# Query projection by seven half-block products in a fused cross-attention and state-space kernel (f32, one core)

## The chip, the cores and the metric

The kernel runs on one core of a Trainium2 chip. The metric is the device time of one execution in microseconds (us); lower is better. The engines have their own instruction streams: PE (TensorE matmuls; PEld is its weight load), DVE (VectorE), ACT (ScalarE), POOL (GpSimd) and SP (SyncE, which issues most DMAs). PE writes into PSUM banks of 128 partitions by 512 f32; ACT and DVE read them from there.

## The reference

One layer over x (4096 queries of width 512) and a context (3202 rows of width 512), with 8 heads of width 64, in f32:

```python
x = _layernorm(builder_state, g1, beta1)
base_n = _layernorm(base_state, g1, beta1)
# _mha: q, k, v = heads(x, Wq, bq), heads(kv, Wk, bk), heads(kv, Wv, bv)
#       attn = softmax(q k^T / sqrt(HD)); out = (attn v) @ W_o.T + b_o
x = residual + _mha(x, base_n, W_qkv, b_qkv, W_o, b_o)
residual = x
xn = _layernorm(x, g2, beta2)
U = (xn @ W_in.T + b_in) @ Bmat
# step: s = silu(s @ A.T) + u_t, over the 4096 steps
x = residual + einsum('tbs,sh->bth', states, Cmat)
return x + (program_probs.mean(axis=1) @ W_prog.T + b_prog)
```

The change concerns `heads(x, Wq, bq)` alone: the 512 by 512 projection of the normalised queries.

## The kernel before

**Stages.** A lead (function `lead`, up to about 200 us of the span) normalises and turns the context, makes all keys and values and stores them in HBM (`kd`, `vd`), and makes the queries of the first block. Then comes the attention over 8 blocks of QB = 512 queries (Q = 0 to 7). Last, a scan over the states runs in chunks, overlapping the last block's end (`drain`).

**A block.** `units` lists (Q, hp, half): hp is one of 4 pairs of heads (128 features), half is 256 queries of the block. A unit has NDC = 13 steps of 256 keys (the last has 128). A step is a set of scores (`scores`, line 1069: 16 matmul instructions of 64 by 64 weights and 256 columns; the array runs four of them side by side), an exponential on ACT (`weights`, line 1146, out into a p tile), a running sum for the denominators on DVE (`add`, line 1154) and, LAG = 4 steps later, a set of value products (`product`, line 1203, into two po banks; the last step has eight instructions more, line 1191). p tiles are a ring of NP = 18; a tile is given back when both its add and its value products are done. At a unit's end DVE folds the sum (1161), ACT swaps halves (1173), DVE gathers (1178), PE sums over partitions (`sums`, pd, 1231), ACT copies the denominators (1270), DVE inverts them (1275), scales the output (1286) and checks the inverse's sum (1278); `output` (ACT, 1248) and `join` (DVE, 1252) take the values out of the po banks. Each pair of heads begins with a bound on its scores from a sample of keys: `sample` (1089), `maximum` (1103), `spread` (1111, PE), `base` (1124, 1125, DVE) and `extra` (ACT, 1131); `rest` (1140, DVE) adds the extra keys to the sum.

**The queries of the next block.** `queries` loads the next 512 rows of x while block Q runs, normalises them, turns them on DVE (`flip`) and by 16 small DMAs on SP (`move`) into the tile `xn` (128 partitions, 4 parts of the 512 features, 512 queries). Four pieces of `heads` then follow, one for a pair of heads: four matmuls of 128 by 128 weights and 512 columns (line 333; f32 takes two instructions each, so 8), then one ACT operation (line 342) that scales, adds the bias and writes a tile of 128 by 512 in the ring `qp` of six. The tile `xn` is free for the next block when all four are done.

**The rows of a block that is done.** `project` makes the output projection (`outs`, pa, line 1446), the residual, the second layer norm and the state inputs (`inputs`, pu, line 1503) of each half block.

**What sets the order.** Nothing is ordered by hand inside the attention. `Plan` holds pieces, each with an engine, an assumed cost, the pieces it comes after, a due time and the rings it takes from and gives back to. `Plan.order` runs a list schedule over assumed costs and emits the pieces in that order; each engine then executes its own instructions strictly in that order, waiting on semaphores. PE's pieces are of two kinds: `"quarters"` (64 by 64 tiles of the array) and whole-array ones. The planner charges ENTER and LEAVE for a change of kind, and holds a lone whole-array piece back by ALONE. `PORT` names DVE's pieces that it keeps off POOL's. Two PSUM banks (`ps_m`, `ps_n`; ring `m` of two) serve the heads, the samples, the denominators, pa and pu in turn.

**Seven products exist already** in the lead: `Seven` (line 500) makes groups of keys and values with them. The sums of weights are made on POOL (`weight_sums`, line 708), the differences of the context tile on DVE (line 735) in four `qp` tiles, the banks are read by ACT (513, 517) and DVE (523).

Of the kernel before, what the change touches and what calls it, by code (L numbers as in the profile page):

```python
# [20 lines left out]
P = 128  # L21
# [20 lines left out]
NP = 18  # L42
# [28 lines left out]
class Plan:  # L71
# [12 lines left out]
    PORT = ("add", "rest", "fold", "gather", "scale", "t", "tied", "wk", "wv", "wq", "rowv")  # L84
# [107 lines left out]
def xattn_ssm_kernel(  # L192
# [118 lines left out]
    qp = actx.enter_context(tc.tile_pool(name="qp", bufs=6))  # L311
# [17 lines left out]
    def heads(Q, hp, xn, home=None):  # L329

        pq = home() if home else m_tile([P, 512], f"pq_{Q}_{hp}")
        for i in range(NC):
            nc.tensor.matmul(  # L333
                pq,
                wq[:, i, hp * P : (hp + 1) * P],
                xn[:, i, :],
                start=(i == 0),
                stop=(i == NC - 1),
            )
        yield  # L340
        t = qp.tile([P, QB], F32, tag="q", name=f"q_{Q}_{hp}")
        nc.scalar.activation(  # L342
            t, pq, AF.Identity, bias=bias[:, hp : hp + 1], scale=HD**-0.5
        )
        qt[Q, hp] = t
# [128 lines left out]
    def quarters(w):  # L474

        lo, hi = slice(0, QU), slice(QU, H)
        return w[:, :2, lo], w[:, 2:, lo], w[:, :2, hi], w[:, 2:, hi]

    class Seven:
# [11 lines left out]
        def product(self, k):  # L491
            if k == "1":
                self.x = self.bank("x")
            elif k == "2":
                self.y = self.bank("y")
            to, left, right = self.y if k in "235" else self.x, self.left[k], self.right[k]
            for b in range(2):
                of = slice(b * P, (b + 1) * P)
                for i in range(2):
                    nc.tensor.matmul(  # L500
                        to[:, b, :],
                        left[:, i, of] if self.of_keys else right[:, i, of],
                        right[:, i, :] if self.of_keys else left[:, i, :],
                        start=(k in "125" and b == 0 and i == 0),
                        stop=(i == 1),
                        skip_group_check=True,
                    )
# [48 lines left out]
    def lead():  # L556
# [3 lines left out]
            dict(cx=6, xh=3, fs=3, t=2, v=2, k=2, m=2, ct=2, q=6, ks=3, vs=3, w=2),  # L560
# [135 lines left out]
        def weight_sums(name, w, tags, after, due):  # L696

            a11, a12, a21, a22 = quarters(w)
            left = dict(zip("124", (a11, a12, a22)))
# [10 lines left out]
            for i, (k, x, y, op) in enumerate((  # L710
                ("5", a21, a22, ALU.add), ("6", "5", a11, ALU.subtract),
                ("7", a11, a21, ALU.subtract), ("3", a12, "6", ALU.subtract),
            )):
                first = {"6": "5", "7": "6", "3": "7"}.get(k)
                add(("s", name, k), "POOL", 1300, partial(sum_, k, x, y, op),
                    after + ([("s", name, first)] if first else []), due + i * 1300)
            return left

        def group(g, lefts):
# [3 lines left out]
            right = {}  # L723
# [4 lines left out]
            def sum_(k):  # L728
# [3 lines left out]
                t = qp.tile([P, QB], F32, tag="q", name=f"t{k}_{g}").rearrange("p (c k) -> p c k", c=2)  # L732
# [4 lines left out]
            for i, k in enumerate("5674"):  # L737
                first = {"6": "5", "4": "6"}.get(k)
                add(("t", g, k), "DVE", 690, partial(sum_, k),
                    halves[0] + halves[1] + ([("t", g, first)] if first else []), d + 3000 + i, ["q"],  # L740
                    [ct] + ([("q", ("t", g, first))] if first else []))
# [7 lines left out]
            for at_, (a, k) in enumerate(  # L749
# [10 lines left out]
                gives = [ct] if k in "123" else [("q", ("t", g, k))]  # L760
# [213 lines left out]
        for hp in range(FIRST):  # L974
            v, d = {}, start_of(n_g) + 10000 + 3000 * hp

            def head(hp=hp, v=v):
# [6 lines left out]
                [("x.copy", t) for t in range(NT)] + ["wq", "wq.bias"], d, ["m", "q"])  # L984
# [72 lines left out]
    sp_ = lctx.enter_context(tc.tile_pool(name="sp_", bufs=NP))  # L1057

# [297 lines left out]
    def queries(plan, Q, d):  # L1356
# [42 lines left out]
        head_pieces(plan, Q, range(NC), w, copied, d, QSTEP // 2, [("xn", of_xn)])  # L1399
# [7 lines left out]
    def head_pieces(plan, Q, hps, xn, copied, d, apart, xn_, ring="m"):  # L1407
# [4 lines left out]
        for hp in hps:  # L1412
# [6 lines left out]
            plan.add(("heads", Q, hp), "PE", 3600, head, copied, d, [ring, "q"], xn_)  # L1419
# [165 lines left out]
    def open_scan():  # L1585

        t = qp.tile([P, QB], F32, tag="q", name="c2")
# [330 lines left out]
    def unit(plan, i):  # L1918
# [17 lines left out]
        q = [("q", Q, hp)] if Q or hp >= FIRST else []  # L1936
        first = i if half == 0 else index[Q, hp, 0]
        if half == 0:
            d = (max(s0 - REF, 0) if i else -40) * STEP
            plan.add(("sample", i), "PE", 440, partial(sample, w), q, d, ["m", "m"],  # L1940
                     [("q", ("heads", Q, hp))], "quarters")
# [8 lines left out]
        for c in range(NDC):  # L1950
# [5 lines left out]
                     [("q", ("heads", Q, hp))], "quarters")  # L1956
# [24 lines left out]
    def drain(plan):  # L1981
# [14 lines left out]
        plan.add("c2", "SP", 200, open_scan, [("heads", NQB - 1, NC - 1)], a0 - 6 * STEP, ["xn", "q"])  # L1996
# [10 lines left out]
        for j in range(L):  # L2007
            plan.add(("fetch", j), "SP", 100, partial(fetch, j),
                     ["fetch", ("product", n, j // 2)], d + (5 + j / 2) * STEP, ["p"])
# [210 lines left out]
    with tc.manual_schedule():  # L2220
# [4 lines left out]
                s=2, m=2, mt=1, o=1, p=NP, acc=3, extra=4, q=6, x=2, x1=1, xn2=1, fs=4,  # L2225
                xn=1, xh=2, max=2, rd=2, o_=12,
            ),
            dict(q=[("heads", 0, hp) for hp in range(FIRST)], xn=["first"]),
        )
        head_pieces(plan, 0, range(FIRST, NC), first_xn, [("spread", 0)], -40 * STEP, 0, [("xn", "first")], "o")  # L2230
# [102 lines left out]
```

## Time and profile before

| | us |
|---|---|
| median of 3 runs | 1921.74 (1921.47 to 1922.03) |
| the profiled execution, its own time | 1919.92 |
| its span in the profile | 1918.0 |
| query heads, line 333, PE busy | 110.5 (248 instructions) |
| query reads, line 342, ACT busy | 21.3 (31) |
| scores and values, lines 1069 and 1203, PE busy | 839.7 and 838.8 |
| output projection, line 1446, PE busy | 107.0 |

How to read it: a group's row gives the source line, engine, operation, out<-in by tile names, partitions x elements, the count, then busy time and mean ns of one, then the idle time of the engine just before these instructions and what ended most of it. Matmuls are pipelined, so the rows of a timeline overlap by the last one's tail; the distance between two starts is the price of one in a stream. In a timeline a row gives start, length, engine, line and how many instructions were merged. Some records of matmuls are missing (a few per cent).

### The profile page before, as it was taken

To read this page: it belongs to the slowest core of one execution; us is meant where nothing else is said; L and a number is where in the kernel's file an instruction comes from. 1 tells how busy PE (TensorE), PEld (TensorE's weight loads), DVE (VectorE), ACT (ScalarE), POOL (GpSimd) and SP (SyncE) were. 2 spreads that over 40 slices of the span, in tenths; PEclk is the share of its full clock that TensorE was granted. 3 is DMA by queue.
4 is the path that set the end of the run, shared out by engine and by line. 5 is a ranking of instruction groups with operands and counts; after the bars stand their busy time and mean duration, and the time that the engine had idled before them with its cause. 6 is when DMAs were issued, how large, how long until landed. Compare 5 with 4: busy or idle time off the path is not lost.

```text
span 1918.0 us, 67581 instructions
## 1 busy us (share of the span) xinstructions
PE 1903.8 (99%) x29296; PEld 1318.5 (69%) x29296; DVE 1502.4 (78%) x2035; ACT 1173.6 (61%) x1647; POOL 231.5 (12%) x378
## 2 busy tenths in 40 slices
PE   9999999999999999999999999999999999999997
PEld 5887688666667666666667666766666666766675
DVE  6642697888868887788778887888788886978877
ACT  3242676676656666656667665666666765766653
POOL 6120000001100120011000120012001110011105
PEclk9999999999999999999999999999999999999999
DMA  7554232232422343223323342224322341545577
GB/s 253 160 155 123 61 105 58 69 103 77 107 71 82 93 125 88 82 75 108 88 59 93 85 126 75 82 87 120 87 68 87 88 123 54 151 117 145 174 191 230
DMA packets 260761, 207.47 MB, mean 108 GB/s; under 512 B 94632, under 2 KB 233896, under 8 KB 260460
## 3 DMA queue, kind: packets, MB, share of 16 engines
q1 hardware_dynamic: 256440, 196.48, 36.1%
q10 hardware_dynamic: 4020, 6.62, 1.2%
q8 instruction: 232, 3.80, 0.8%
q14 instruction: 69, 0.57, 0.1%
HBM read 156.32 MB, written 29.88 MB: 97 GB/s over the span
## 4 chain that ended last, share of the span: by engine, by line


## 5 line engine op out<-in xcount | busy, mean ns | idle before, releaser
L1146 ACT ACTIVATE p<-s,shifts 128x1024 f32<-128x1024 f32 (+1 forms) x832 | 893.1, 1082 | 477.7 <-PE s L1069 462.4
L1154 DVE TENSOR_TENSOR acc<-p,acc 128x1024 f32<-128x1024 f32 (+1 forms) x704 | 828.3, 1177 | 136.9 <-ACT p L1146 101.8
L1069 PE MATMUL s<-q,k 64*64 64x256 f32 x12800 | 839.7, 377 | 0.2 <-ACT p L1146 0.2
L1203 PE MATMUL po<-p,v 64*64 64x256 f32 x12800 | 838.8, 377 | 0.0
L1069 PEld LDWEIGHTS s<-q,k 64*64 64x64 f32 x12800 | 500.4, 133 | 199.2 <-ACT p L1146 15.0
L1203 PEld LDWEIGHTS po<-p,v 64*64 64x64 f32 x12800 | 497.9, 133 | 184.3 <-issue 17.3
L1275 DVE RECIPROCAL rd<-rd 128x256 f32<-128x256 f32 (+1 forms) x64 | 110.1, 1722 | 70.6 <-ACT rd L1270 70.6
L1440 POOL TENSOR_TENSOR xr<-xr,rowb 128x512 f32<-128x512 f32 x30 | 40.7, 1365 | 996.9 <-DMA k<-kd 422.6
L333 PE MATMUL pq<-xn,wq 128*128 128x512 f32 x248 | 110.5, 598 | 0.0
L1446 PE MATMUL pa<-wo,o 128*128 128x512 f32 x240 | 107.0, 599 | 0.0
L1154 DVE TENSOR_TENSOR acc<-p,p 128x1024 f32<-128x1024 f32 x64 | 80.3, 1254 | 10.2 <-ACT p L1146 9.9
L333 PEld LDWEIGHTS pq<-xn,wq 128*128 128x128 f32 x248 | 45.8, 190 | 55.8 <-issue 55.8
L1446 PEld LDWEIGHTS pa<-wo,o 128*128 128x128 f32 x240 | 44.4, 190 | 56.0 <-issue 56.0
L342 ACT ACTIVATE q<-pq,bias 128x512 f32<-128x512 f32 x31 | 21.3, 687 | 84.3 <-PE pq L333 84.3
L1178 DVE TENSOR_TENSOR acc<-swap,acc 64x256 f32<-64x256 f32 x126 | 55.3, 439 | 8.9 <-ACT swap L1173 7.2
L1140 DVE TENSOR_TENSOR acc<-x,acc 2x256 f32<-2x256 f32 x128 | 53.1, 415 | 2.6
L1173 ACT COPY swap<-acc 64x256 f32<-64x256 f32 x126 | 50.8, 404 | 6.9 <-DVE acc L1161 3.2
L1463 POOL TENSOR_TENSOR xr<-x,modb 128x512 f32<-128x512 f32 x30 | 38.2, 1273 | 121.4 <-DVE x L1459 121.4
L1161 DVE TENSOR_TENSOR acc<-acc 128x512 f32<-128x512 f32 x63 | 44.2, 701 | 1.4
L1336 POOL TENSOR_SCALAR rstd_x<-mv_x 128x1 f32<-128x1 f32 x28 | 6.2, 220 | 319.1 <-DVE mv_x L1333 317.5
L523 DVE TENSOR_TENSOR ks<-pky,ks 128x512 f32<-128x512 f32 x15 | 10.4, 692 | 43.6 <-PE pky L500 28.7
L517 ACT ACTIVATE ks<-pkx,bias 128x256 f32<-128x256 f32 x40 | 16.8, 471 | 43.1 <-PE pkx L500 31.6
(260 smaller groups left out, 1405.8 us busy)
## 6 DMA issues: line engine op xcount, KB each, us to landing
k<-kd SPq DMA_DIRECT2D x432, 128.0 KB, 2.5
v<-vd SPq DMA_DIRECT2D x432, 128.0 KB, 2.2
xn<-x SPq DMA_DIRECT2D x448, 32.0 KB, 1.9
xr<-in_x_dram SPq DMA_DIRECT2D x30, 256.0 KB, 3.2
x1d<-xr SPq DMA_DIRECT2D x30, 256.0 KB, 2.3
x<-in_x_dram SPq DMA_DIRECT2D x28, 256.0 KB, 3.7
cx<-in_ctx_dram SPq DMA_DIRECT2D x25, 256.0 KB, 4.9
kd<-ks SPq DMA_DIRECT2D x20, 256.0 KB, 2.3
```

What stands on the lines that cost most here:

```text
L333: nc.tensor.matmul(pq, wq[:, i, hp * P : (hp + 1) * P], xn[:, i, :], start=(i == 0), stop=(i == NC - 1),)
L1069: nc.tensor.matmul(s[k0 : k0 + HD, a, b, :], kts[(*w["at"][:2], c)][r, b * CK + k0 : b * CK + k0 + HD], q[r], start=True, stop=True, skip_ ...
L1140: nc.vector.tensor_tensor(to[r], t[r], to[r], ALU.add)
L1146: nc.scalar.activation(t[:, :, :nb, :], w["ps"][c][:, :, :nb, :], AF.Exp, bias=w["shift"])
L1154: nc.vector.tensor_tensor(w["acc"][:, :, :nb, :], t[:, :, :nb, :], before[:, :, :nb, :], ALU.add)
L1161: nc.vector.tensor_tensor(acc[:, :, 0, :], acc[:, :, 0, :], acc[:, :, 1, :], ALU.add)
L1173: nc.scalar.copy(w["swap"][r], of[(1 - k) * HD : (2 - k) * HD])
L1178: nc.vector.tensor_tensor(of[r], w["swap"][r], of[r], ALU.add)
L1203: nc.tensor.matmul(w["po"][k][a * HD : (a + 1) * HD, :QU], vts[Q, hp, c][r, b, a * HD : (a + 1) * HD], t[r, a, b, :], start=(c == 0 and b ...
L1275: nc.vector.reciprocal(w["rd"][:, part], (w["pd"] if last else w["rd"])[:, part])
L1440: nc.gpsimd.tensor_tensor(v["x"], v["x"], rowb, ALU.add)
L1446: nc.tensor.matmul(v["pa"], o_t[Q, c, half][:, t * P : (t + 1) * P], wo[:, c, :], start=(c == 0), stop=(c == NC - 1),)
```

## The change

For blocks Q = 1 to 7, the four pieces of `heads` become seven products of half size, one level of Strassen's scheme in Winograd's form. With a = the query weights in quarters (a11, a12: first two pairs of heads, by halves of the features; a21, a22: last two pairs), and b = `xn` in quarters (b11, b21: first 256 queries, by halves of the features; b12, b22: last 256):

- sums of weights, once, on POOL: s5 = a21 + a22, s6 = s5 - a11, s7 = a11 - a21, s3 = a12 - s6
- differences per block, on DVE: t5 = b12 - b11, t6 = b22 - t5, t7 = b22 - b12, t4 = b21 - t6; t7 overwrites b12 and t4 overwrites b21 in `xn`
- products in the order 1, 2, 6, 5, 7, 3, 4, into two banks: x gathers a11 b11, then s6 t6, s7 t7, a22 t4; y takes a12 b21, is begun anew with s5 t5, then gathers s3 b22
- after each product the bank is read out, before the next may write it: x after 1, 6, 4 and y after 5 by ACT (two operations of 128 by 256, with scale and bias), y after 2 and 3 and x after 7 by DVE (one operation that scales and adds onto the query tile in SBUF)

A product is four matmuls (eight instructions) of 128 by 128 weights and 256 columns. The query tiles become tiles of two pairs of heads (128 by 2 by 512), in a ring of three; the lead's differences share them two by two. Three tiles `alt` hold the weight sums (two) and t5, t6 (one), and later serve as rows 0 to 2 of the last stage; for them the ring of p tiles goes from 18 to 15. The two banks of ring `m` are held from product 1 to the last reads.

In the built order of instructions, PE's stream in the lead and behind the last block's queries is the same as before. In blocks three to eight the three heads that stood right behind pu are gone from there; products 1, 2 and 6 come where the fourth head stood, behind score set 5 of unit (3,0), then one value set, then 5, 7, 3 and 4. In block two the three heads stood by themselves, between value and score sets of unit (2,1); its products stand where the others do. On DVE t5, t6 and t7 stand near score sets 2 and 3 of unit (2,1), t4 and the three reads among the adds of unit (3,0). The load of Cmat for the scan (`c2`) comes 17 rows later on SP.

```diff
-NP = 18
+NP = 15
+NA = 3
...
-    qp = actx.enter_context(tc.tile_pool(name="qp", bufs=6))
+    qp = actx.enter_context(tc.tile_pool(name="qp", bufs=3))
...
+    def pair_of(Q, hp):
+        t = qp.tile([P, 2, QB], F32, tag="q", name=f"q_{Q}_{hp}")
+        for k in range(2):
+            qt[Q, hp + k] = t[:, k]
+        return t
...
+    def seventh(to, still, moving, start):
+        for b in range(2):
+            for i in range(2):
+                nc.tensor.matmul(
+                    to[:, b, :],
+                    still[:, i, b * P : (b + 1) * P],
+                    moving[:, i, :],
+                    start=(start and b == 0 and i == 0),
+                    stop=(i == 1),
+                    skip_group_check=True,
+                )
+
+    def left_sums(w):
+        a11, a12, a21, a22 = quarters(w)
+        return (
+            ("5", a21, a22, ALU.add), ("6", "5", a11, ALU.subtract),
+            ("7", a11, a21, ALU.subtract), ("3", a12, "6", ALU.subtract),
+        ), dict(zip("124", (a11, a12, a22)))
...
-        head_pieces(plan, Q, range(NC), w, copied, d, QSTEP // 2, [("xn", of_xn)])
+        by_sevenths(plan, Q, w, copied, d, ("xn", of_xn))
+
+    lefts = {}
+
+    def query_weights(plan, after, d):
+        sums, left = left_sums(wq)
+        lefts["q"], tiles = left, {}
+        def sum_(k, x, y, op):
+            if k in "57":
+                tiles[k] = parts_of(alt_tile("57".index(k), f"sq{k}"))
+            left[k] = tiles["57"[k in "73"]][k in "63"]
+            x, y = (left[z] if isinstance(z, str) else z for z in (x, y))
+            nc.gpsimd.tensor_tensor(left[k], x, y, op)
...
+    CHAIN = "1265734"
+    READS = {
+        "1": ("11", "ACT"), "2": ("11", "DVE"), "6": ("12", "ACT"), "5": ("22", "ACT"),
+        "7": ("22", "DVE"), "3": ("12", "DVE"), "4": ("21", "ACT"),
+    }
+
+    def by_sevenths(plan, Q, w, copied, d, of_xn):
...
+        def sum_(k):
...
+            x, y = {"5": (b12, right["1"]), "6": (b22, right["5"]), "7": (b22, b12), "4": (b21, right["6"])}[k]
+            nc.vector.tensor_tensor(right[k], x, y, ALU.subtract)
...
+            seventh(v["y" if k in "235" else "x"], left[k], right[k], k in "125")
+
+        def read(k):
+            m, n = READS[k][0]
+            of, cs = v["y" if k in "235" else "x"], slice((int(n) - 1) * QU, int(n) * QU)
+            t = to[m][:, :, cs]
+            if READS[k][1] == "DVE":
+                nc.vector.scalar_tensor_tensor(t, of, HD**-0.5, t, ALU.mult, ALU.add)
+                return
+            for b in range(2):
+                hp = (int(m) - 1) * 2 + b
+                nc.scalar.activation(
+                    t[:, b], of[:, b], AF.Identity, bias=bias[:, hp : hp + 1], scale=HD**-0.5
+                )
...
+        before = {"6": "1", "5": "2", "7": "6", "3": "5", "4": "7"}
+        needs = {"1": copied + [("sq", "3")], "2": copied + [(*key, "1")], "3": copied}
+        for at, k in enumerate(CHAIN):
+            after = needs.get(k, [("tq", Q, k)]) + ([("sevenths.read", Q, before[k])] if k in before else [])
+            gives = [("tq", ("tq", Q, "5"))] if k in "56" else [of_xn]
+            plan.add((*key, k), "PE", 1740, partial(product_, k), after,
+                     d + at - (plan.ALONE if at > 1 else 0),
+                     {"1": ["m", "m", "q"], "5": ["q"]}.get(k, []), gives)
...
-            rows[j] = sp_.tile([P, 2, H], F32, tag="s", name=f"row_{j}")
+            rows[j] = alt_tile(j, name) if j < NA else sp_.tile([P, 2, H], F32, tag="s", name=name)
```

More of the change, by code (lines that the diff above doesn't have):

```diff
@@ L83 @@
     ENDS = 2 * NC * NQB - 2
-    PORT = ("add", "rest", "fold", "gather", "scale", "t", "tied", "wk", "wv", "wq", "rowv")
+    PORT = ("add", "rest", "fold", "gather", "scale", "t", "tq", "tied", "wk", "wv", "wq", "rowv")
     SHIFT = {
@@ L495, in product @@
                 self.y = self.bank("y")
[L496 to L507, printed above, removed]
+            to, sides = self.y if k in "235" else self.x, [self.left[k], self.right[k]]
+            seventh(to, *(sides if self.of_keys else sides[::-1]), k in "125")
         def keep(self, k, half):
@@ L696, in weight_sums @@
         def weight_sums(name, w, tags, after, due):
[L698 to L699 removed]
+            sums, left = left_sums(w)
             tiles = {}
```

102 lines of the change are left out of this document (75 added, 27 removed).

## The prediction

> **What bounds the kernel now.** I read the page first, then the stretches of one block, then the instructions of TensorE (PE) in order of time.
>
> ```profile
> span 1918.0 us, 67581 instructions
> PE 1903.8 (99%) x29296; PEld 1318.5 (69%) x29296; DVE 1502.4 (78%) x2035; ACT 1173.6 (61%) x1647; POOL 231.5 (12%) x378
> ...
> L1146 ACT ACTIVATE p<-s,shifts 128x1024 f32<-128x1024 f32 (+1 forms) x832 | 893.1, 1082 | 477.7 <-PE s L1069 462.4
> L1069 PE MATMUL s<-q,k 64*64 64x256 f32 x12800 | 839.7, 377 | 0.2 <-ACT p L1146 0.2
> ...
> L333 PE MATMUL pq<-xn,wq 128*128 128x512 f32 x248 | 110.5, 598 | 0.0
> ...
> L1463 POOL TENSOR_TENSOR xr<-x,modb 128x512 f32<-128x512 f32 x30 | 38.2, 1273 | 121.4 <-DVE x L1459 121.4
> ...
> L517 ACT ACTIVATE ks<-pkx,bias 128x256 f32<-128x256 f32 x40 | 16.8, 471 | 43.1 <-PE pkx L500 31.6
> ```
>
> PE is busy in 99% of the span. Its two largest users wait 0.2 us in all for others, whereas ScalarE's exponentials (L1146) wait 462.4 us for PE. So engines wait for PE, not PE for them. One block of 512 queries repeats every 210 us, and two windows confirm that other engines have room inside it:
>
> ```profile
> 541.00:560.00 19.00, 19.00 (x365) 13.41 (x360) 16.70 (x21) 13.65 (x22) 0.00 (x0) 1.00 0.38 112
> 560.00:770.00 210.00, 210.00 (x3489) 140.95 (x3490) 172.67 (x221) 136.78 (x185) 20.49 (x32) 1.00 0.32 90
> ```
>
> The columns are PE, PEld, DVE, ACT and POOL: in 210 us VectorE (DVE) works 172.67, ScalarE (ACT) 136.78, GpSimd (POOL) 20.49; the next column is PE's granted clock, 1.00 of full speed. A microsecond taken off PE's stream inside a block is a microsecond off the end, as long as PE finds its operands ready. That condition is what has to be worked out.
>
> **What the matmuls cost.** A busy time includes the tail of a pipelined matmul, so I price by distance from start to start. Before the change, block 3's query heads stand like this on PE:
>
> ```profile
> 528.58 1.09 PE L1503 MATMUL pu<-xn,wc 128*64 128x128 f32 x16
> 529.60 10.57 PE L333 MATMUL pq<-xn,wq 128*128 128x512 f32 x24
> 540.10 1.09 PE L1203 MATMUL po<-p,v 64*64 64x256 f32 x16
> 541.02 0.40 PE L1231 MATMUL pd<-acc,ones 64*64 64x128 f32 x8
> 541.23 1.04 PE L1069 MATMUL s<-q,k 64*64 64x256 f32 x16
> 542.10 1.04 PE L1203 MATMUL po<-p,v 64*64 64x256 f32 x16
> ...
> 558.07 1.91 PE L1069 MATMUL s<-q,k 64*64 64x256 f32 x32
> 559.91 3.70 PE L333 MATMUL pq<-xn,wq 128*128 128x512 f32 x8
> 563.54 1.74 PE L1203 MATMUL po<-p,v 64*64 64x256 f32 x28
> ```
>
> Three pairs of heads take 529.60 to 540.10 = 10.50, one alone 559.91 to 563.54 = 3.63. The two added ones are therefore 6.87/2 = 3.435 each, and leaving a group of full-array matmuls costs 3.63 - 3.435 = 0.195. A regular set of scores takes 541.23 to 542.10, 0.864 when averaged over a longer stretch, so two sets from 558.07 end at 559.80 and entering a group costs 0.11. The first set behind a group takes 0.92 (540.10 to 541.02), 0.055 more than usual. A block's heads now cost 4 x 3.435 = 13.74 plus their entries and exits.
>
> The new half-block product (four matmuls of 256 columns, eight instructions) already exists in the lead, at line 500, also accumulating:
>
> ```profile
> 54.52 1.89 PE L500 MATMUL pky<-t,sk 128*128 128x256 f32 x8
> ...
> 59.70 1.89 PE L500 MATMUL pvx<-sv,t 128*128 128x256 f32 x8
> ...
> L500 PEld LDWEIGHTS pvx<-wv,t 128*128 128x128 f32 x40 | 7.5, 190 | 1.0
> ```
>
> 54.52 to 59.70 is three products without a gap (that of 54.52 and two left out): 1.727 each. Seven are 12.09. Bounds: half a pair's 3.435 from below (7 x 1.717 = 12.02), the busy time 1.89 from above (13.23). I take 1.727, the same instructions in the same succession. Gain per block: 13.74 - 12.09 = 1.65.
>
> A row first, then a rule against the change: a weight load takes 190 ns here and one instruction of 256 columns starts every 1.727/8 = 0.216 us, one of 512 columns every 3.435/8 = 0.429. The added 256 columns cost 0.213, so the load lies wholly under the streaming. The Trainium skill ("TensorE: Matmul & The Clock Gate", section "Measured speedup vs the span model") says that a weight load overlaps matmuls in flight only when their row group differs. By it, 56 loads in place of 32 would each stand on the path, and the sum would turn into a loss (last rival). By that rule the trace does not agree.
>
> **Groups.** In the built order the three heads behind pu (the state inputs) are gone from there in blocks three to eight. Instead, behind score set 5 of unit (3,0), where the fourth head stood, come products 1, 2, 6, then one value product (po), then 5, 7, 3, 4. So pu becomes a group by itself. It costs 1.02 before pq and 1.02 before scores, so its exit is paid either way:
>
> ```profile
> 478.15 1.09 PE L1503 MATMUL pu<-xn,wc 128*64 128x128 f32 x16
> 479.17 1.09 PE L1069 MATMUL s<-q,k 64*64 64x256 f32 x16
> ```
>
> What is added is one entry and one slow first set, 0.11 + 0.055 = 0.165, at most a whole 0.36 (with an exit of 0.195), at least nothing. Block two has no pu before its heads: two groups before, two after. Sum on PE: 7 x 1.65 - 6 x 0.165 = 10.56 us.
>
> **Does PE find its operands?** Count from T, the start of product 1. Product 6 overwrites the bank that ACT reads after product 1, so it waits. Product 1's matmuls end at 1.89. ACT may still be busy with the exponentials of sets 4 and 5:
>
> ```profile
> 559.19 2.12 ACT L1146 ACTIVATE p<-s,shifts 128x1024 f32<-128x1024 f32 x2
> 563.65 0.69 ACT L342 ACTIVATE q<-pq,bias 128x512 f32<-128x512 f32 x1 [2.34 <-PE pq L333]
> ```
>
> With pq's start at 559.91 as T they end at 561.31, T + 1.40, and ACT starts 0.04 after PE's end (563.61 to 563.65). Two reads of 471 ns (L517's) end at T + 2.88; product 6 is due at T + 3.45. 0.57 to spare; queued behind those reads is the swap, then the read of 6. Nothing waits there unless ACT is late by more than that.
>
> The tighter one is product 5, which starts bank y anew and needs DVE's read of product 2. It is due after products 1, 2, 6 (5.18), an exit 0.195, one po 0.92 and an entry 0.11: T + 6.40. On DVE, in order, everything between the base of unit (3,0) and this read stands ahead of it. Its rows:
>
> ```profile
> 525.69 0.29 PE L1111 MATMUL sm<-twice,m 64*64 64x64 f32 x8
> ...
> 526.50 0.68 DVE L1161 TENSOR_TENSOR acc<-acc 128x512 f32<-128x512 f32 x1
> 527.11 2.48 DVE L1154 TENSOR_TENSOR acc<-p,acc 128x1024 f32<-128x1024 f32 x2
> ...
> 542.18 1.75 DVE L1275 RECIPROCAL rd<-rd 128x256 f32<-128x256 f32 x1 [7.98 <-ACT rd L1270]
> ...
> 544.64 3.87 DVE L1154 TENSOR_TENSOR acc<-p,acc 128x1024 f32<-128x1024 f32 x3
> ...
> 553.99 0.68 DVE L1154 TENSOR_TENSOR acc<-p,acc 128x512 f32<-128x512 f32 x1
> 554.71 0.69 DVE L1161 TENSOR_TENSOR acc<-acc 128x512 f32<-128x512 f32 x1
> 555.37 1.23 DVE L1154 TENSOR_TENSOR acc<-p,p 128x1024 f32<-128x1024 f32 x1
> 556.51 0.84 DVE L1178 TENSOR_TENSOR acc<-swap,acc 64x256 f32<-64x256 f32 x2
> 557.37 0.84 DVE L1140 TENSOR_TENSOR acc<-x,acc 2x256 f32<-2x256 f32 x2
> 558.31 1.23 DVE L1154 TENSOR_TENSOR acc<-p,acc 128x1024 f32<-128x1024 f32 x1
> 559.46 0.42 DVE L1252 TENSOR_TENSOR o<-po,o 128x256 f32<-128x256 f32 x1
> 559.79 3.87 DVE L1154 TENSOR_TENSOR acc<-p,acc 128x1024 f32<-128x1024 f32 x3
> ...
> L735 DVE TENSOR_TENSOR t<-ct,t 128x512 f32<-128x512 f32 x10 | 6.9, 688 | 0.2
> L523 DVE TENSOR_TENSOR ks<-pky,ks 128x512 f32<-128x512 f32 x15 | 10.4, 692 | 43.6 <-PE pky L500 28.7
> ```
>
> From start to start: an add in a row 3.87/3 = 1.29, the half add 0.72, the fold 0.66, the add of two tiles 1.14, a gather 0.86, the rest 0.94, the join 0.33, a reciprocal with scale and sum 2.46 (542.18 to 544.64). A new difference is 0.69 (L735), a read of a bank with an add into SBUF 0.69 (L523). After the change the stretch holds 12 adds in a row (15.48), one of two tiles 1.14, the half add 0.72, two folds 1.32, one gather 0.86, two reciprocal sets 4.92, rest 0.94, join 0.33, four differences 2.76 and the read 0.69: 29.16 us. The first fold starts 0.81 after the spread on PE (525.69 to 526.50). From the spread to T PE does 24 sets (20.74), a half set 0.43, the last value set 0.65, two pd 0.43 (0.21 each, 541.02 to 541.23), pu with its entry 1.19, the spread 0.12 and the entry 0.11: 23.67. So the fold starts at T - 22.86. The read ends at T + 6.30, and PE needs it at T + 6.40. Adds that come in twos take 1.24 each (2.48/2), by which 12 of them would leave 0.7; a few late semaphores eat that. I take no stall; between a spare half microsecond and a lateness of 1 us both ends stay in the range. The old three-head stop at 529.60 let DVE catch up by 7.98 us here; that cover is gone, which is why it is so close. Behind the waiting PE stand the next value and score sets, so every late tenth is on the path.
>
> The read of 7, due at T + 11.5 before product 4, has 1.5 us after product 7's end at T + 10; the reads of 6 and 5 on ACT have over half a microsecond, as no score set comes in between.
>
> **The smaller edits.** DVE gains seven operations of 0.69 per block, 4.8 us on 172.67 of 210: not the bound. ACT has eight half reads for four whole ones: about 1 us on 136.78. The four weight sums on POOL come once, in the first unit, beside adds with a slack of many sets; were the cover gone, some 5 us once (four of the size of L1463's, 1.27). Three p tiles fewer: exponentials never waited for a tile (L1146 waits for scores). A tile is held for about four score sets on PE (LAG in the code) and, by the sum above, at most some 11 us on DVE; 15 tiles last 15 x 1.73 = 26 us, so nothing, and were it short, each late add would stop an exponential and then PE. Pair tiles in a ring of three hold as much as six single ones; PE's order in the lead and behind the last block is unchanged, and Cmat's load, now later on SP, is wanted only by the closing scan: nothing.
>
> **Sum.** 10.56 off the span of 1918.0 gives 1907.4; the profiled execution's own 1919.92 becomes 1909.4; the median of the runs, 1921.74, lies 1.82 above it, so 1911.2.
>
> **Rivals.**
> B, the read of product 2 is late by 0.6 to 1.2 us in each block: for it the margin of 0.1; against it the shorter paired adds. Stall about 0.7 x 7 = 5: 1916.
> C, the gain is given back, that is, the change doesn't do on the clock what it says: DVE sets the block's length. For it 85% of the block filled; against it 31 us still free per block. 1921.7.
> D, slower: the same read is late by more than 2.2 us (from there 7 stalls exceed 10.56 + 3.8). It would take all 12 adds at 1.48 in place of 1.29, as when POOL shares the port; against it, POOL has 0.00 in 541 to 560. With 2.4 us: 7 x 2.3 = 16, 1927.
> E, weight loads on the path: 56 x (0.190 + 0.213) = 22.6 against 32 x (0.190 + 0.427) = 19.7 per block, 20 us more: 1942. Against it the 0.429 measured where it would be 0.617.
>
> **How the numbers follow.** Forecast 0.68, B 0.17, C 0.06, D 0.08, E 0.01. The lower end is the cheapest product and no extra entry, 12.0 off: 1909.7. The upper end takes B in, to 0.9 us a block: 1917.5. Together 0.84. Faster by over 0.2% (3.8 us, about what a measurement here tells from no change) means below 1917.9: the forecast and most of B, 0.83. Within: C and the rest of B, 0.08. Slower: D and E, 0.09.
>
> **What would show it.** Seven products in a block in 3 + 4 with 1.73 us from start to start, PE without idle time before product 5, and a block period of 208.4. Idle PE before product 5, released by DVE's read of y, is B or D by its size; idle before product 6 released by ACT would mean that the ACT step is wrong. Products further apart than 1.75 refute the price; a block still at 210 without idle PE refutes the sum. Exponentials waiting for adds would refute the argument on the p ring.

## The result and the profile after

| | before | after |
|---|---|---|
| median of five runs beside each other | 1922.03 us (1921.47 to 1925.62) | 1913.58 us (1911.67 to 1914.29) |
| profiled execution, its span | 1918.0 us | 1911.7 us |
| block period on PE, a block without a stall | 209.89 us | 208.47 us |

The ratio is 0.9949, with a 95% interval of 0.9935 to 0.9964: 8.45 us less, in the predicted range and 2.4 us above the predicted time. The next set of five runs of the same kernel had a median of 1911.98 us, the ratio there 0.9945 (0.9931 to 0.9959).

The page of the changed kernel, the rows that answer to those of before:

```profile
span 1911.7 us, 68126 instructions
PE 1895.2 (99%) x29464; PEld 1352.6 (71%) x29464; DVE 1535.3 (80%) x2084; ACT 1176.6 (62%) x1675; POOL 237.7 (12%) x382
...
L1172 ACT ACTIVATE p<-s,shifts 128x1024 f32<-128x1024 f32 (+1 forms) x832 | 892.9, 1082 | 481.1 <-PE s L1095 464.0
...
L1095 PE MATMUL s<-q,k 64*64 64x256 f32 x12800 | 837.4, 377 | 0.2 <-ACT p L1172 0.2
```

PE still is the bound. The exponentials wait nearly always for scores (464.0 of 481.1 us), and in no case for an add or a value product, the two that give a p tile back: in this execution the ring of 15 tiles holds nothing up. The products of block three (1, 2, 6, a value set, 5, 7; products 3 and 4 are left out) and the first output projection (pa) of two blocks in PE's timeline:

```profile
547.47 1.99 PE L364 MATMUL qx<-xn,wq 128*128 128x256 f32 x8
549.30 1.89 PE L364 MATMUL qy<-xn,wq 128*128 128x256 f32 x8
551.03 1.89 PE L364 MATMUL qx<-tq,sq 128*128 128x256 f32 x8
552.85 1.09 PE L1229 MATMUL po<-p,v 64*64 64x256 f32 x16
553.87 1.99 PE L364 MATMUL qy<-tq,sq 128*128 128x256 f32 x8
555.71 1.89 PE L364 MATMUL qx<-xn,sq 128*128 128x256 f32 x8
...
636.31 1.55 PE L1561 MATMUL pa<-wo,o 128*128 128x512 f32 x3
...
844.78 1.55 PE L1561 MATMUL pa<-wo,o 128*128 128x512 f32 x3
```

Products start 1.73 apart (1.83 behind a group's first), in groups of 3 and 4; product 5 starts 6.40 after product 1, to the hundredth where the prediction had it, and a block is 844.78 - 636.31 = 208.47 long. In the profile before the same two pa rows stand at 639.66 and 849.55. The break into two groups shows in the rows: product 6, the value set and product 5 take 1.82, 1.02 and 1.84 to the next start, in place of 1.73, 0.86 and 1.73 inside a group, 0.36 together.

What the prediction did not have is in the list of PE's waits:

```profile
PE qy L364 <- DVE q L1487: 1.2, 1, 1.2
...
PE pu L1618 <- DMA xn<-x: 0.9, 1, 0.9
```

(microseconds, times, longest). Once in seven blocks product 5 waits for VectorE, and the update stage waits for its copies.

**Where the stall comes from.** VectorE's timeline in the undisturbed block three, fold, first sum (for product 5), sum for product 4, read of product 2:

```profile
524.57 0.69 DVE L1187 TENSOR_TENSOR acc<-acc 128x512 f32<-128x512 f32 x1
...
526.30 0.69 DVE L1468 TENSOR_TENSOR tq<-xn 128x512 f32<-128x512 f32 x1
...
551.23 0.69 DVE L1468 TENSOR_TENSOR xn<-xn,tq 128x512 f32<-128x512 f32 x1
551.84 0.68 DVE L1487 SCALAR_TENSOR_TENSOR q<-qy,q 128x512 f32<-128x512 f32 x1
```

With T = 547.47 the first sum starts at T - 21.17, the read ends at T + 5.05: 1.35 to spare before product 5. The same in block six, where product 1 starts at T = 1172.89, with the issue of the copies of xn by SyncE (a half block takes 16 of them; the row has the last 15 of the second half) and PE's row:

```profile
1139.35 12.09 SPq L453 DMA_DIRECT2D xn<-x  x15
...
1154.46 0.69 DVE L1468 TENSOR_TENSOR tq<-xn 128x512 f32<-128x512 f32 x1 [2.66 <-DMA xn<-x]
...
1179.24 0.69 DVE L1468 TENSOR_TENSOR xn<-xn,tq 128x512 f32<-128x512 f32 x1
1179.85 0.68 DVE L1487 SCALAR_TENSOR_TENSOR q<-qy,q 128x512 f32<-128x512 f32 x1
...
1180.59 1.78 PE L364 MATMUL qy<-tq,sq 128*128 128x256 f32 x7 [1.23 <-DVE q L1487]
```

The issue of the last copy ends at 1151.44, T - 21.45. The first sum needs the data, waits 2.66 us and starts at T - 18.43, which is 2.74 later than in block three. VectorE has no idle time of note from there on, so the read ends at T + 7.64, 2.59 later. The 1.35 to spare are eaten and the rest, 1.23, stands on PE. Nearly thirty operations lie between the two, over 25 us, and almost nothing of the lateness is made up.

That was the theory to test (A). Its rival (B) was a read that is late in itself, whatever the copies do. Two other blocks of this execution bear on it: their first sums wait 0.73 and 1.07 us for a copy and start 0.82 and 1.16 later than in block three, which is less than there is to spare, and their product 5 starts at T + 6.41, on time.

### The profile page after: what moved, and what is told of

It reads as the page before. It is cut to its first block, busy times and chain, and to the rows that moved or that the text cites. A ratio compares the mean times of both kernels' runs of the same rounds, so it can differ in the third digit from the quotient of the medians.

```text
span 1911.7 us, 68126 instructions
## 1 busy us (share of the span) xinstructions
PE 1895.2 (99%) x29464; PEld 1352.6 (71%) x29464; DVE 1535.3 (80%) x2084; ACT 1176.6 (62%) x1675; POOL 237.7 (12%) x382
## 4 chain that ended last, share of the span: by engine, by line
## 5 line engine op out<-in xcount | busy, mean ns | idle before, releaser
L1172 ACT ACTIVATE p<-s,shifts 128x1024 f32<-128x1024 f32 (+1 forms) x832 | 892.9, 1082 | 481.1 <-PE s L1095 464.0
L1491 ACT ACTIVATE q<-qx,bias 128x256 f32<-128x256 f32 x42 | 17.6, 471 | 45.8 <-PE qx L364 45.8
L542 DVE TENSOR_TENSOR ks<-pky,ks 128x512 f32<-128x512 f32 x15 | 10.4, 692 | 43.6 <-PE pky L364 28.7
L1278 DVE TENSOR_TENSOR o<-po,o 128x256 f32<-128x256 f32 x64 | 27.0, 421 | 12.3 <-ACT o L1274 7.6
L1129 DVE TENSOR_REDUCE m<-sm 128x1 f32<-128x256 f32 x64 | 24.1, 419 | 15.7 <-PE sm L1115 15.2
```

The lines of the kernel that those rows point to most:

```text
L1172: nc.scalar.activation(t[:, :, :nb, :], w["ps"][c][:, :, :nb, :], AF.Exp, bias=w["shift"])
```

## The experiments

The runs of this section were made in three sets on three chips. The kernel before, run beside each set, had medians of 1921.92, 1921.75 and 1922.03 us, so that times are compared across them.

**The changed kernel itself, once more.** 

> The changed kernel once more, beside its variants. Two theories of where the gain stands. A: the seven products gain the predicted 10.6 us of PE time, and of it about 1.3 us come back where a product 5 waits for VectorE behind a late copy of xn, 0.7 to 0.9 us at a wait of the update stage for its own copy, and 1.8 us where the granted clock falls to a half for 3.4 us near the end. Then one run to the next differs by which of these it meets: spans of 1909 to 1913 us, and each stall before a product 5 has a VectorE wait for a copy of xn of over 2 us some 20 us ahead of it. B: the loss sits in the blocks themselves (a read of product 2 that is late in each block, or the ring of 15 score tiles). Then every block of 208.5 us has idle PE before product 5, the same in this run as in the one before.

Measured: 1911.98 us (1910.39 to 1913.21), profiled span 1910.5. It has one stall again, in another block:

```profile
528.51 0.69 DVE L1468 TENSOR_TENSOR tq<-xn 128x512 f32<-128x512 f32 x1 [2.23 <-DMA xn<-x]
...
554.63 1.56 PE L364 MATMUL qy<-tq,sq 128*128 128x256 f32 x6 [0.78 <-DVE q L1487]
...
1649.68 0.34 PE L1137 MATMUL sm<-twice,m 64*64 64x64 f32 x8 [1.05 <-DVE m L1130]
```

The stall is in block three, which was undisturbed in the other execution. So the stall belongs to a late copy, not to a block. B's idle PE in each block is not there. PE's longest wait in the attention is another one here: the spread of the last block (line 1137) waits 1.05 us for the maximum on VectorE, where an add of two tiles took 2.19 us in place of 1.23 and a step of the maximum 1.17 in place of 0.16. Why single operations of VectorE take a microsecond longer now and then was not looked for.

**The copies late on purpose.** The last copies are issued twice (same data), once with the sums where the change has them and once with three of them later:

```diff
-                move(w["xn"][:, :, half * QU : (half + 1) * QU], v["x"], a)
+                for _ in range(2 if half and a == P // TB - 1 else 1):
+                    move(w["xn"][:, :, half * QU : (half + 1) * QU], v["x"], a)
```

> The last four copies into xn of each block of queries are issued a second time, with the same data, some 2.5 us more on the queue of SyncE ahead of the sums; the rest as in the changed kernel. A (a late copy holds up the first sum on VectorE, all that stands behind it, the read of product 2 and so product 5): the first sum starts 2 to 3 us later in blocks that had no room, its lateness beyond 1.35 us arrives at product 5, and the median rises by 3 to 10 us above the changed kernel. B (late copies are caught up on the way, the stall seen was something else): 0 to 1 us.

Measured: 1924.58 us (1922.17 to 1929.66), 12.6 above the changed kernel's 1911.98; ratio to before 1.0014 (1.0004 to 1.0023). Block three on SyncE, VectorE and PE, and the waits of product 5 in all blocks:

```profile
513.04 14.68 SPq L453 DMA_DIRECT2D xn<-x  x20
...
530.47 0.69 DVE L1469 TENSOR_TENSOR tq<-xn 128x512 f32<-128x512 f32 x1 [4.01 <-issue]
...
555.84 0.68 DVE L1488 SCALAR_TENSOR_TENSOR q<-qy,q 128x512 f32<-128x512 f32 x1
...
556.58 3.60 PE L364 MATMUL qy<-tq,sq 128*128 128x256 f32 x8 [2.55 <-DVE q L1488]
560.01 1.89 PE L364 MATMUL qx<-xn,sq 128*128 128x256 f32 x8
```

```profile
PE qy L364 <- DVE q L1488: 9.8, 6, 2.8
```

The copies are issued until 527.72, 3.25 us later than in the changed kernel's block three (the profile found no releaser for the sum's wait and calls it issue). A is right, and the price is above its 10 us: six of seven blocks stall, 9.8 us in all. The lateness arrives one for one. In these six blocks, and in the one stalled block of each of the two executions above, the first sum starts 2.26 to 4.31 us later than T - 21.17, and product 5 starts later than T + 6.40 by that lateness less 1.44 to 1.46. In the ten unstalled blocks, three to eight, of those two executions the sum is at most 1.18 late, and product 5 at most 0.01. In block three of the present run product 5 itself takes 560.01 - 556.58 = 3.43 in place of 1.83. That is the clock, below.

The sums for 5, 6 and 7 later, without and with the copies twice:

```diff
-            plan.add(("tq", Q, k), "DVE", 690, partial(sum_, k), after, d - 2 * STEP,
...
+            plan.add(("tq", Q, k), "DVE", 690, partial(sum_, k), after, d + 8 * STEP if k in "567" else d - 2 * STEP,
...
```

> The sums for products 5, 6 and 7 come about 17 us later on VectorE, behind its add of the twelfth score tile; PE's order stays. A: they no longer wait for a copy of xn, no product 5 is late, and the median falls by 0 to 1.5 us beside the changed kernel; the read of product 2 still ends about 5.05 us after the start of product 1, because VectorE does the same work in that stretch. B (the read itself is tight, since VectorE is full there): the sums stand nearer to the read, it ends later by up to 2 us, and product 5 waits in each block: 0.7 us and more in each of 7, the median 4 us and more above the changed kernel.

> The same four copies twice, with the sums for products 5, 6 and 7 about 17 us later, as in the run with the late sums. A: no sum waits for a copy, the read of product 2 ends about 5.2 us after the start of product 1 in each block, and the time is that of the run with the late sums, 1912 us within 1 us. B (the longer queue itself costs the time, by late loads of k and v): as much above it as the kernel with the copies twice is above the changed kernel.

Measured: 1912.25 us (1911.75 to 1914.25), ratio 0.9950 (0.9937 to 0.9964), and with the copies twice 1912.69 us (1911.07 to 1913.44), ratio 0.9953 (0.9937 to 0.9968). Block three of the latter:

```profile
513.13 14.81 SPq L453 DMA_DIRECT2D xn<-x  x20
...
544.37 0.69 DVE L1469 TENSOR_TENSOR tq<-xn 128x512 f32<-128x512 f32 x1
...
552.24 0.68 DVE L1488 SCALAR_TENSOR_TENSOR q<-qy,q 128x512 f32<-128x512 f32 x1
...
554.11 1.99 PE L364 MATMUL qy<-tq,sq 128*128 128x256 f32 x8
```

The copies are as long on the queue, 14.8 us, yet neither the sum nor product 5 waits; the read ends at 552.92, 5.21 after product 1 (547.71). The same twenty copies thus cost 12.6 us or under one, by where the sums stand. The long queue itself costs nothing that can be told, so B falls. With the plain copies the late sums did not lower the median: no product 5 waits in the profile (0.78 us in the run beside it, span 1909.9 against 1910.5), though the spread of the last block waits 1.00 us again. One stall of a microsecond a run is no more than the runs differ by.

**How much room the read has.** The sum for product 7 five times:

```diff
-            nc.vector.tensor_tensor(right[k], x, y, ALU.subtract)
+            for _ in range(5 if k == "7" else 1):
+                nc.vector.tensor_tensor(right[k], x, y, ALU.subtract)
```

> The sum for product 7 is done five times in place of once (in place, so that an odd count gives the same value): four more operations of 0.61 us, 2.44 us more VectorE work ahead of the read of product 2, the rest unchanged. A (the read has 1.35 us to spare, not the 0.1 us of the prediction, and VectorE is full from the sums to the read, so that each microsecond of delay arrives there): the read ends about 7.5 us after the start of product 1, product 5 starts 1.1 us late in an undisturbed block, more where a copy of xn is late too: 7 x 1.1 = 7.7 to 11 us above the changed kernel, 1920 to 1924. The prediction's margin of 0.1 us: 7 x 2.35 = 16.5 us, about 1929. C (VectorE has slack in that stretch and catches up): no change.

Measured: 1930.95 us (1927.49 to 1933.77), ratio 1.0046 (1.0031 to 1.0061), 19 us above the changed kernel. The total is nearer to the figure from the margin of 0.1 us, but the rows are not. Block five, with no late copy, and block four, with one (VectorE's sum, then PE's product 5 and what follows):

```profile
958.12 3.59 DVE L1469 TENSOR_TENSOR xn<-xn 128x512 f32<-128x512 f32 x5
...
985.02 1.99 PE L364 MATMUL qy<-tq,sq 128*128 128x256 f32 x8 [1.02 <-DVE q L1488]
...
742.80 0.69 DVE L1469 TENSOR_TENSOR tq<-xn 128x512 f32<-128x512 f32 x1 [1.60 <-DMA xn<-x]
...
772.18 3.78 PE L364 MATMUL qy<-tq,sq 128*128 128x256 f32 x8 [3.42 <-DVE q L1488]
775.75 3.05 PE L364 MATMUL qx<-xn,sq 128*128 128x256 f32 x8
```

Without a late copy product 5 waits 1.02, as the room of 1.35 has it; a margin of 0.1 would have made it over 2.3. A repeated sum took 3.59/5 = 0.72, not 0.61; each works on the result of the one before, which may be why. In block five the first sum starts at T - 21.52, 0.35 early: 4 x 0.72 - 0.35 - 1.45 = 1.08, and product 5 is 1.09 late. What I had not counted is the other blocks: product 5 starts 8.55, 8.89, 9.89, 7.49, 8.40, 8.12 and 7.84 after product 1 in place of 6.40, 14.4 us in all (in block two most of it stands ahead of product 6 already), and after the two longest waits products cost up to 3.57 us (772.18 to 775.75) in place of 1.83. VectorE with 2.9 us more to do is late in all seven blocks; PE pays for it by waiting, and in two blocks by a slower clock as well.

**What a stall of PE costs beyond itself.** The windows view, each time one stretch of 3.41 us and the next one; the granted clock changes at their boundaries (columns: PE, PEld, DVE, ACT, POOL busy, PE's granted clock, DMA share, GB/s). First the block just shown:

```profile
767.86:771.27 3.41, 0.91 (x16) 0.33 (x11) 3.38 (x4) 1.64 (x4) 0.00 (x0) 1.00 0.00 0
771.27:774.68 3.41, 2.50 (x6) 2.05 (x7) 3.31 (x6) 0.00 (x0) 0.00 (x0) 0.50 0.02 5
```

Then the closing scan of the changed kernel's first execution, and of its repeat:

```profile
1867.42:1870.83 3.41, 1.52 (x12) 1.03 (x12) 2.89 (x7) 0.98 (x3) 2.64 (x3) 1.00 0.87 214
1870.83:1874.24 3.41, 3.41 (x22) 2.77 (x20) 0.80 (x3) 0.86 (x2) 1.38 (x3) 0.50 0.43 162
```

```profile
1866.08:1869.49 3.41, 2.18 (x16) 0.88 (x12) 3.17 (x10) 0.55 (x2) 1.59 (x3) 1.00 1.05 231
1869.49:1872.90 3.41, 2.48 (x26) 1.93 (x25) 1.70 (x4) 1.35 (x3) 2.99 (x4) 1.00 1.06 237
```

After a stretch in which PE was busy for 0.91 or 1.52 us, the next one has half the clock; after 2.18 it has not. In the scan PE waits the same 1.21 and 0.93 us in both executions. In the first both waits fall into one stretch, and the next 3.41 us run at half the clock; in the repeat the boundary at 1869.49 lies between them, and the clock stays. From the last pa to the end the first takes 138.79 us, the repeat 137.24. The scan of all twelve profiles of this study fits: where these waits leave 1.52 to 1.83 us of busy PE in one stretch, half the clock follows (four executions); where 1.93 to 2.28 are left, it does not (eight). The boundaries lie elsewhere in the program from one execution to the next. The Trainium skill ("TensorE: Matmul & The Clock Gate", section "What's actually happening") says that the window is 3413 ns long and runs freely, without a new start when a kernel starts. The stretches here agree.

So it differs between executions of one and the same kernel. The next run looks at the kernel before.

> The kernel before once more, for the clock and the waits of its own runs. A (the granted clock's half-speed stretches near the end fall where a wait of PE lies within one 3.41 us stretch, and that is chance, whatever the kernel): some of its runs have clock 0.999 and some 0.998, with 1.7 to 2 us between them, and its last wait of the update stage for its copies (0.26 us in the profile before) is anything from 0.2 to 1.7 us. B (the changed kernel brings these losses): all runs at 0.999, and that wait stays at 0.3 us.

Measured: 1921.78 us (1920.94 to 1922.53), ratio 0.9999 (0.9990 to 1.0008). Six of its eleven runs have a clock of 0.998 or less, as all of the changed kernel's first five and one of its next five had. So the kernel before has stretches at half clock too, as A has it, and B falls; but the 1.7 to 2 us between such runs are not there (median span 1919.5 at 0.999, 1920.0 below it). What the mean clock shows is not what was lost: in this run's profile it is 0.998 because the half clock begins one stretch earlier at the very end, at 1909.56 + 3.41 = 1912.97, and none falls into the scan. That a kernel with whole heads can lose in the scan as well is shown by the first run with four whole heads, below (1.74 us busy from 1878.01 on, then half the clock); for the kernel before no profile shows it. The update stage (line 1503, later 1618: pu, the state inputs) waits 0.53 us in it, between the first two profiles. Their rows, before and after:

```profile
1726.53 1.09 PE L1503 MATMUL pu<-xn,wc 128*64 128x128 f32 x16 [0.26 <-issue]
```

```profile
1718.42 1.09 PE L1618 MATMUL pu<-xn,wc 128*64 128x128 f32 x16 [0.95 <-DMA xn<-x]
```

**The rest of the change alone.** Pair tiles, ring of 15 and GpSimd's sums stay, the queries are four whole heads. Two lines of the edit are left out: the heads take the query tiles, and the load of Cmat waits for the last head.

```diff
-        by_sevenths(plan, Q, w, copied, d, ("xn", of_xn))
+        head_pieces(plan, Q, range(NC), w, copied, d, QSTEP // 2, [("xn", of_xn)])
...
-            of_q = ("sevenths", Q, "15"[hp // 2])
-            q = [("sevenths.read", Q, k) for k in ("23", "74")[hp // 2]]
+            of_q = ("heads", Q, hp // 2 * 2)
+            q = [("q", Q, hp)]
```

> All of the change stays (pair tiles, three of them, the ring of 15 score tiles, the sums of wq on GpSimd), but the queries of blocks two to eight are computed by four whole heads again, eight half-block products. A (the whole gain is the price of the products, the rest costs nothing): block period 209.9 us as before, span 1918 us, or 1920 if the clock falls to a half near the end; median 1920 to 1923. B (the smaller ring or the fewer tiles cost something, which the products' gain hides): median 1924 or more, with idle PE before scores or exponentials that the kernel before does not have.

> The run with four whole heads once more, for its waits in the last block. A (its 2 us over the kernel before are the wait of the update stage for its copies, 1.7 us there, and that is a matter of when the copies' issues are held up): that wait is shorter this time, 0.3 to 1 us, and the profiled span is 1 us nearer to the kernel before. B (the ring of 15, the pair tiles or the moved loads of the scan bring it each time): the wait is 1.5 us and more again, and the median is 1923.5 or more.

Measured: 1924.12 us (1922.15 to 1926.15) and 1923.33 us (1922.05 to 1927.82), ratios 1.0009 (1.0000 to 1.0018) and 1.0010 (1.0001 to 1.0019). The wait of the update stage (pu) in the last block of each:

```profile
1728.51 1.09 PE L1618 MATMUL pu<-xn,wc 128*64 128x128 f32 x16 [1.69 <-DMA xn<-x]
```

```profile
1728.41 1.09 PE L1618 MATMUL pu<-xn,wc 128*64 128x128 f32 x16 [0.42 <-ACT p L1172]
```

The rest costs 1.3 to 2.2 us beside the kernel before, near the edge of what can be told, and not by that wait alone: it was short the second time (as A has it), the median nearly as high (B's side of the line in the first, just under it in the second). A block is 209.95 long, 0.07 more than before. By the starts of the exponentials both executions run within 0.9 us of the first one of the kernel before up to the last block, and fall behind by 1.3 and 2.3 us in its last units; the second execution of the kernel before falls behind by 0.5 there. Which part of the rest does it was not tried. The gain is then all the products' own: without them the time is 1923.3 to 1924.1 us, with them about 1912.

**One group in place of two.** The sum for product 4 goes behind the read of product 2 as well, alone, or together with the late sums:

```diff
-            plan.add(("tq", Q, k), "DVE", 690, partial(sum_, k), after, d - 2 * STEP,
...
+            plan.add(("tq", Q, k), "DVE", 690, partial(sum_, k), after, d + 10 if k == "4" else d - 2 * STEP,
...
+            plan.add(("tq", Q, k), "DVE", 690, partial(sum_, k), after, d + 8 * STEP if k in "567" else d + 10,
...
```

> Only the sum for product 4 moves, behind the read of product 2 on VectorE; the sums for 5, 6 and 7 stay early, as in the changed kernel. All seven products of blocks three to eight then stand in one group. A (one group entry of 0.36 us less in each of six blocks, and late copies of xn still reach product 5): 6 x 0.36 = 2.2 us below the changed kernel, about 1910; the read ends at about 4.4 us in an undisturbed block and product 5 starts at 5.28, so that a first sum more than 0.9 us late stalls product 5, in one or two blocks of a run. B (the gain of the run with one group came from the late sums): median within 0.7 us of the changed kernel, 1911.5 to 1912.5.

> As the run with the late sums, and the sum for product 4 goes behind the read of product 2 on VectorE, so that blocks three to eight do all seven products in one group, as planned by the due times. The prediction charged 0.165 us for the second group in each of six blocks, and product 1's entry. A: the group's entry is 0.16 to 0.36 us, the median is 1.0 to 2.2 us below the run with the late sums, and product 5 (now due about 5.2 us after the start of product 1) does not wait, since the read ends at about 4.4 us. B (the group of two hid something: VectorE or the score tiles need the pause): product 5 or an exponential waits, and the median is equal or higher.

Measured: alone 1911.54 us (1909.14 to 1912.66), ratio 0.9943 (0.9929 to 0.9956); with the late sums 1909.61 us (1908.32 to 1910.31), ratio 0.9931 (0.9917 to 0.9944). Block three of the latter, products 6, 5 and 7, and two pa:

```profile
551.35 1.89 PE L364 MATMUL qx<-tq,sq 128*128 128x256 f32 x8
553.08 1.89 PE L364 MATMUL qy<-tq,sq 128*128 128x256 f32 x8
554.80 1.89 PE L364 MATMUL qx<-xn,sq 128*128 128x256 f32 x8
...
636.27 1.98 PE L1561 MATMUL pa<-wo,o 128*128 128x512 f32 x4
...
844.38 1.98 PE L1561 MATMUL pa<-wo,o 128*128 128x512 f32 x4
```

Product 5 follows product 6 after 1.73, without a wait, and a block is 208.11 long, 0.36 less than with two groups. Together they give the lowest median of this study, 2.4 us below the changed kernel's 1911.98 and 2.64 below the late sums, somewhat beyond A's 1.0 to 2.2; that product 5 does not wait is as A had it. Alone, the later sum for 4 leaves the early sums waiting for copies, and one block of that execution stalls by 0.34. Its median is in B's range and can't be told from the changed kernel's. Its profile speaks for A, though: the blocks without a stall are 208.11 long, and the span, 1907.4, is the shortest of all profiles. The five runs differ by 3.5 us, more than the 2.2 in question, so the median does not settle it; the rows show the same gain per block.

## Why the prediction was right

- **The price of the products: right.** They start 1.73 apart, as the rows of the lead had it, although 56 weight loads took the place of 32. The rule of the Trainium skill by which it would have been a loss (rival E) fell with that; the page "TensorE: Matmul & The Clock Gate" has it in the section "The mechanism", not in the one that the prediction names. One block gives 209.89 - 208.47 = 1.42, where the prediction's 1.65 - 0.165 is 1.485; in one group it gives 209.89 - 208.11 = 1.78. So seven products were worth a little more than 1.65, and the second group 0.36, the upper bound in place of the 0.165 taken. A group's entry, exit and slow first set are all paid once more, as the rows of product 6, the value set and product 5 show; no exit was "paid either way". The two errors nearly cancel, which is luck: with six blocks at 1.42 and 1.95 ahead of block three (a pa at 427.84 against 429.79, up to 0.4 of it there before the products) the attention part gains 10.1 to 10.5 of the predicted 10.56, where nothing stalls.
- **The step that failed: the operands.** "I take no stall" rested on a sum over VectorE's stretch from the fold to the read of product 2, in which each operation starts when the one before it ends. The first sum in that stretch has an input of its own, the last copy of xn, and that was never held against a time. Before the change only the heads on PE needed it, some three microseconds later. The sums on VectorE, which work in order, bring that wait to the head of everything between them and the read. The sum itself was on the safe side: the read ends at T + 5.05, not T + 6.30, as four adds in a row took 1.245 each and the differences about 0.61. Had it been 0.1 as predicted, each late copy would have counted in full.
- **ACT ahead of product 6, the reads of 7, 6 and 5, the p ring: right by the waits.** No product but the fifth waits in the changed kernel, and no exponential waits for a tile. That the smaller edits together cost nothing is not borne out: with whole heads in their place they cost 1.3 to 2.2 us, from a part that was not found.
- **The sum against the median.** In the two profiled executions the span falls by 6.3 us. From 10.4 come off the stall, 1.23, the update stage's wait, 0.95 against 0.26 us, and up to 1.7 for the stretch at half clock which the execution before did not have: 10.4 - 1.2 - 0.7 - 1.7 = 6.8, the remaining 0.5 not assigned. The 1.82 us between the execution before and the median were carried over as a constant, though single runs of that kernel lie between 1919.89 and 1925.31 in one set; what made up the 1.82 is not known. That the forecast of the median holds to 2.4 us owes something to luck.
- **The rivals.** B had the right place and size of a stall (0.6 to 1.2), but it is one block in seven and not each. A read that is later than its margin in nearly all blocks, as D has it, came only with the five sums and the double copies, by more work and later data and not by slower adds. It then costs more than its length, up to 1.7 us where half the clock follows for a stretch. C falls with the block of 208.47, E with the products' distance of 1.73.

## What to carry to other kernels

When work moves to an in-order engine that is full for a long stretch, look up when each new input lands, not only whether the work fits: here a wait at the head of a full stretch arrived nearly undiminished at its end, 25 us later, and what exceeded the room there stood on PE. Put such work as late as its own consumer allows; the same operations 18 us later were immune to copies that otherwise cost 12.6 us. When PE stalls, ask whether a stretch at half clock can follow, and add what it costs.

## What was not expected of the hardware

- PE's clock can drop already when less than half of one 3.41 us stretch is idle, and busy time alone does not tell when. Two stretches of the execution with five sums, each with the one after it:

```profile
1402.74:1406.15 3.41, 1.76 (x20) 0.95 (x19) 3.35 (x6) 1.06 (x3) 0.00 (x0) 1.00 0.00 0
1406.15:1409.56 3.41, 3.41 (x18) 3.00 (x17) 2.75 (x4) 0.84 (x2) 0.00 (x0) 1.00 0.00 0
1918.15:1921.56 3.41, 1.91 (x22) 1.22 (x20) 2.22 (x7) 0.91 (x4) 1.26 (x1) 1.00 0.94 311
1921.56:1924.97 3.41, 2.21 (x10) 0.60 (x10) 2.25 (x8) 0.24 (x2) 0.00 (x0) 0.50 0.49 162
```

  In the scan 1.91 us busy lost the full clock and 1.93 kept it, in one and the same execution; in the attention 1.76 kept it. What the clock goes by besides is not shown here.
- Issues of copies on SyncE, usually 0.6 us each, were now and then about a microsecond longer (42 of 448 took over 0.85 us in the changed kernel). That makes a last copy late, but it is not all: in blocks six and seven the last issue ends at T - 21.45 and T - 21.52, and the first sum starts at T - 18.43 and T - 20.01. In block six the data also landed later, 2.8 us after the issue's end, where 1.3 is usual. The causes were not looked for.
